# A fifth block product of a first layer computed from sub-blocks, rows fetched whole, and weighting moved from VectorE

## The chip, the cores and the metric

The kernel runs on one core of one Trainium2 chip. The metric is the device time of one execution in microseconds, as the median of several runs. Beside it stands one execution recorded by the hardware profiler, from which all rows here are taken.

## The reference

A batch of 4096 tokens of 512 numbers (`x`) is rotated, routed and sent through a mixture of eight experts, and the result is added back to `x`.

```
x_rotated = hamilton(q_left, hamilton(filter(x), conj(q_right)))   # 4 parts of 128 per token
logits = x_rotated @ gate_w.T ; top 2 of 8 experts, gates from the two scores
disp = each expert's first 1024 tokens, in order (8 x 1024 x 512)
h  = relu(disp @ fc1_w.T + fc1_b)        # 512 -> 2048, per expert
eo = h @ fc2_w + fc2_b                   # 2048 -> 512
out = x + sum over the two choices of gate * eo[expert, place]
```

All of it is float32. Nearly all arithmetic is in the two matrix products of each expert.

## The kernel before, in words

**Blocks.** A prologue on the whole batch finds for every one of the 64 groups of 128 expert slots which token sits in each slot (`slot_tok`), where its result goes (`slot_add`) and where its gates lie (`slot_cho`). After that the work is 32 blocks, k = 0 to 31: expert e = k // 4, and g = k % 4, a quarter of the 2048 hidden units. In a block the first layer makes 512 hidden units for 1024 slots, and the second layer multiplies them by 512 rows of the second weights and adds into the accumulators `acc`.

**Seven products for eight.** Both layers cut each matrix product in 2 by 2 blocks and use a Strassen-like scheme: seven block products, numbered 0 to 6, in place of eight, for which GpSimd and VectorE make sums of blocks ahead (`left1` L132 for weights, `Slots.factors` L772 for tokens, `right2` L177 for second weights, `chain` L810 for hidden units, four VectorE instructions L819, L822, L823, L824). In the first layer (`layer1`, L844) block products 1, 6, 3 and 2 are again made of seven products of their own quarter blocks (`within`, L833, 128x256 each), from sums made by `left_sub` (L146, GpSimd) and `right_sub` (L162, VectorE). They come in pairs (`pair`, L876): PE writes one sub-product of each of two block products into the two halves of a PSUM bank, and VectorE adds both halves to two of the blocks `h11`, `h21`, `r12`, `h22` at once (L890, L903, L909). Block products 0, 5 and 4 are plain there (`half`, L854: four matmuls of 128x512 each, L856). Block 0 (k = 0) is plain in the first layer (`layer1_plain`, L938).

**Order.** The order of instructions is written by hand. `first_layers` (L980) and `second_layers` (L1119) are generators, each of which does one unit of work and yields; a block has 14 units of each. The main loop (L1242) takes one unit of the first layer, calls `turn`, takes one unit of the second layer, calls `turn`. `first_layers` is started ten units earlier, so the second layer of a block runs in the units of the next block. `turn` (L788) pops as many steps from the list `background` as the table `PACE` (L1229) says for that unit, and one step from the list `fetches`. When one generator has ended, `continue` at L1246 skips its `turn`. In the first layer PE's banks come from `ps_1` (four), in the second from `ps_2` (three). Each engine works through its own queue in order.

**Rows in and out.** The tokens of the next expert are fetched by GpSimd as quarters: `gather_quarters` (L706), an indirect DMA of 128 pieces of 512 bytes, 32 of them for an expert, through the table `quarter` (L103, made at L343 to L350, L568 to L576 and L585). They land so that VectorE can turn 32x32 squares of them (`turn_squares`, L725) and rotate them (L768 on ScalarE, L770 on VectorE) as `background`. They begin at (g, i) = (0, 12) and (1, 12), and the rotation at (1, 11) and (2, 9) (L1094, L1096). Results go back per group of 128 slots (`Rows`, L643): `gather_rows` fetches the present rows of `out`, `weigh` (L671, one VectorE instruction L673, 128x512) multiplies `acc` by the gate and adds the row, `scatter` (L675) writes the row by indirect DMA. A gather from `out` that stands behind a scatter into it waits for the scatter. Weights are loaded by SP's queue, `load_w1(k + 1)` and `load_w2(k + 1)` at the start of block k (L1029).

**The end.** After the last block of the first layer only second-layer units are left. There the fetches of `out` rows, the stores of the first four groups and the last matmuls (L1195 to L1206) lie behind one another.

Of the kernel before, what the change touches and what calls it, by code (L numbers as in the profile page):

```python
# [64 lines left out]
def kernel(  # L66
# [36 lines left out]
    quarter = const.tile([P, NS, QT], I32, name="quarter")  # L103
# [96 lines left out]
    with ExitStack() as rctx:  # L200
# [117 lines left out]
        for k in range(K):  # L318
# [24 lines left out]
        spread = rp.tile([P, QT, QT, CW], F32, name="spread")  # L343
        V.tensor_copy(
            spread,
            ident.rearrange("p (q w) -> p q w", w=CW).unsqueeze(2).to_broadcast([P, QT, QT, CW]),
        )
        base = rp.tile([P, 1], F32, name="base")
        for c in range(QT):
            V.memset(base[c * CW : (c + 1) * CW], float(c * N))  # L350

# [216 lines left out]
        quarter_ps = bank(rps, "rank", NT + 1)[:, : QT * NS].rearrange("p (q s) -> p q s", q=QT)  # L568
        for c in range(QT):
            nc.tensor.matmul(  # L570
                quarter_ps[:, c],
                lhsT=spread[:, c].rearrange("p q w -> p (q w)"),
                rhs=tokf,
                start=True,
                stop=True,
            )  # L576

# [6 lines left out]

        V.tensor_scalar(quarter.rearrange("p s q -> p q s"), quarter_ps, base, None, ALU.add)  # L585
# [13 lines left out]
    vp = ctx.enter_context(tc.tile_pool(name="vp", bufs=3))  # L599
# [43 lines left out]
    class Rows:  # L643
# [43 lines left out]
        def store(self, st, acc):  # L687
            self.weigh(st, acc)
            self.scatter(st)

    class Slots:
# [14 lines left out]
        def gather_quarters(self, half, st, q):  # L706

            if q == 0:
                assert self.e == 1 or STORED[half * PER + st] in stored[self.e - 2]
            s = self.e * SLOTS + half * PER + st  # L710
            nc.gpsimd.indirect_dma_start(  # L711
                out=slots_of[half][:, st, q * P : (q + 1) * P],
                out_offset=None,
                in_=xq,
                in_offset=bass.IndirectOffsetOnAxis(ap=quarter[:, s, q : q + 1], axis=0),
            )

        def quarters(self, half):
            return [
                lambda st=st, q=q: self.gather_quarters(half, st, q)  # L720
                for st in range(PER)
                for q in range(QT)
            ]
# [86 lines left out]
    def chain(k, h22):  # L810
# [6 lines left out]
        def last():  # L817
# [6 lines left out]
            lambda: V.scalar_tensor_tensor(r12, r12, 0.0, h11, ALU.max, ALU.subtract),  # L824
            last,
# [18 lines left out]
    def layer1(k, factors, subs):  # L844
# [20 lines left out]
        for m in range(2):  # L865
            half(a[m], m, 0, True)
            nc.scalar.activation(h11[:, m], a[m], AF.Identity, bias=lo[:, m : m + 1])
            yield
        for m in range(2):
            half(a[m], m, 5, False)  # L870
            nc.scalar.activation(r12[:, m], a[m], AF.Identity, bias=lo[:, m : m + 1])
            if m == 1:
                nc.scalar.activation(h21[:, m], a[m], AF.Identity, bias=hi[:, m : m + 1])
            yield

        def pair(n, o, at, base, base_read):  # L876
# [3 lines left out]
            two = h[:, at : at + 2]  # L880
            t, u = bank1(f"t{n}_{k}"), bank1(f"u{n}_{k}")
            halves = t.rearrange("p (n s) -> p n s", n=2)

            def both(bank, i, first=False):
                within(bank[:, A], subs, n, i, first)
                within(bank[:, B], subs, o, i)

            def add(m, half):
                to = two[:, :, m, half]
                V.tensor_tensor(to, halves, to, ALU.add)  # L890

# [344 lines left out]
    with tc.manual_schedule():  # L1236
# [5 lines left out]
        while going:  # L1242
            going = False
            for n, gen in enumerate((first, second)):
                if next(gen, "end") == "end":
                    continue  # L1246
# [51 lines left out]
```

## Time and profile before

| | |
|---|---|
| median of 3 runs | 1574.2 us (1571.47 to 1574.38) |
| the profiled execution's own time | 1572.69 us |
| its span, first to last instruction | 1570.9 us |
| PE (matmuls) busy | 1531.7 us, 98% |
| VectorE (DVE) busy | 1195.8 us, 76% |
| GpSimd (POOL) busy | 1146.5 us, 73% |
| ScalarE (ACT) busy | 280.9 us, 18% |
| mean granted TensorE clock | 0.985 |

The page gives for a group of instructions its line, engine and operation, what is written and read, how many there are, their busy time, the mean duration of one in ns, and after a bar how long the engine stood idle just before them and what ended that. A float32 matmul in the kernel's text appears as two instructions of PE. Matmuls overlap, so a mean duration is longer than the distance between two starts; costs of PE are therefore taken from distances between starts. DMA is the mean busy share of the 16 DMA engines.

### The profile page before, as it was taken

What the parts mean: (1) busy time and instruction counts of PE and PEld (TensorE: products, weight loads), DVE (VectorE), ACT (ScalarE), POOL (GpSimd) and SP (SyncE); (2) the same over time, 40 slices, a digit from 0 to 9 for tenths busy, and PEclk for the clock granted to TensorE, in tenths of its full rate; (3) what the DMA queues carried; (4) which work ended last, traced back from release to release, by engine and by line L of the source; (5) the groups of instructions that cost most, each with busy time, mean ns of one, the idle gap of its engine ahead of it and who ended that gap; (6) DMA issues with size and microseconds to landing.
All of it is one profiled execution on the core that took longest, in us unless ns stands there. A gap on an engine that the chain in (4) does not pass through costs nothing.

```text
span 1570.9 us, 17111 instructions
## 1 busy us (share of the span) xinstructions
PE 1531.7 (98%) x6407; PEld 1191.2 (76%) x6407; DVE 1195.8 (76%) x1667; ACT 280.9 (18%) x390; POOL 1146.5 (73%) x1241
## 2 busy tenths in 40 slices
PE   5899999999999999999999999999999999999995
PEld 3677877877777887777787787787777788778774
DVE  6567887688876788778886888768887688876663
ACT  3222211221112111122111221122111211111100
POOL 1786686876978777887778868687697877764633
PEclk7899999999999999999999999999999999999998
DMA  8452112321321113321043211222132111321002
GB/s 324 158 174 79 55 53 95 104 77 55 110 98 59 63 54 121 113 86 45 20 141 107 81 55 64 85 103 77 54 114 95 64 53 55 121 100 54 28 8 98
DMA packets 48010, 137.46 MB, mean 88 GB/s; under 512 B 9334, under 2 KB 9590, under 8 KB 42808
## 3 DMA queue, kind: packets, MB, share of 16 engines
q1 hardware_dynamic: 22800, 75.54, 13.0%
q0 software_dynamic: 20736, 52.32, 10.5%
q10 hardware_dynamic: 4392, 8.52, 1.4%
q8 instruction: 50, 0.82, 0.2%
q14 instruction: 32, 0.26, 0.1%
HBM read 119.77 MB, written 25.23 MB: 92 GB/s over the span
## 4 chain that ended last, share of the span: by engine, by line
PE 94%; DMA 2%; issue 1%; DVE 1%; POOL 1%; SPq 0%; POOLq 0%; DVEq 0%
PE a L799 27%; PE b L799 20%; PE t L835 14%; PE a L856 14%; PE u L835 7%; PE b L856 7%; PE p L957 2%; PE b L835 2%; PE a L835 2%; DMA xb<-in_xt_dram 1%; DMA rows<-out_dram,slot_tok 1%; POOL rows L622 1%; POOL out_dram L678 0%; DMA rows<-in_x_dram,slot_tok 0%; SPq L216 0%
## 5 line engine op out<-in xcount | busy, mean ns | idle before, releaser
L711 POOL DMA_INDIRECT rows<-in_xq_dram,quarter x224 | 243.4, 1087 | 55.5 <-issue 48.5
L799 PE MATMUL a<-t,hidden 128*128 128x256 f32 x1024 | 243.9, 381 | 9.7 <-DVE v L1185 9.6
L799 PEld LDWEIGHTS a<-t,hidden 128*128 128x128 f32 x1024 | 195.5, 191 | 63.2 <-issue 27.3
L890 DVE TENSOR_TENSOR beside<-t,beside 128x512 f32<-128x512 f32 x248 | 170.2, 686 | 74.7 <-PE t L835 72.5
L831 ACT ACTIVATE beside<-beside 128x1024 f32<-128x1024 f32 x62 | 65.5, 1057 | 583.4 <-DVE beside L890 583.4
L835 PE MATMUL t<-xsub,sub 128*128 128x256 f32 x496 | 127.3, 379 | 0.0
L799 PEld LDWEIGHTS b<-w,hidden 128*128 128x128 f32 x504 | 95.8, 190 | 39.0 <-issue 28.9
L799 PE MATMUL b<-w,beside 128*128 128x256 f32 x512 | 121.0, 379 | 1.5 <-DVE acc L1208 1.5
L799 PE MATMUL a<-w,beside 128*128 128x256 f32 x512 | 121.0, 379 | 0.0
L799 PE MATMUL a<-t,beside 128*128 128x256 f32 x512 | 120.9, 379 | 0.0
L799 PE MATMUL b<-w,hidden 128*128 128x256 f32 x504 | 119.1, 379 | 0.0
L799 PE MATMUL b<-t,hidden 128*128 128x256 f32 x504 | 119.1, 379 | 0.0
L799 PEld LDWEIGHTS b<-w,beside 128*128 128x128 f32 x512 | 97.2, 190 | 28.3 <-issue 16.7
L799 PEld LDWEIGHTS a<-w,beside 128*128 128x128 f32 x512 | 97.3, 190 | 26.5 <-issue 14.8
L856 PE MATMUL a<-x,s 128*128 128x512 f32 x248 | 116.5, 592 | 0.0
L856 PE MATMUL b<-x,s 128*128 128x512 f32 x248 | 116.5, 592 | 0.0
L856 PE MATMUL a<-xa,w 128*128 128x512 f32 x248 | 116.4, 592 | 0.0
L799 PEld LDWEIGHTS a<-t,beside 128*128 128x128 f32 x512 | 97.3, 190 | 13.2
L678 POOL DMA_INDIRECT out_dram<-rows,slot_add x64 | 64.5, 1007 | 57.2 <-DVE rows L673 44.4
L799 PEld LDWEIGHTS b<-t,hidden 128*128 128x128 f32 x504 | 95.8, 190 | 13.0
L835 PEld LDWEIGHTS t<-xsub,sub 128*128 128x128 f32 x496 | 94.2, 190 | 12.8
L137 POOL TENSOR_TENSOR s<-w 128x512 f32<-128x512 f32 x31 | 39.5, 1274 | 79.4 <-PE b L856 79.4
(235 smaller groups left out, 2965.4 us busy)
## 6 DMA issues: line engine op xcount, KB each, us to landing
w<-in_w_dram SPq DMA_DIRECT2D x64, 1024.0 KB, 7.8
xb<-in_xt_dram SPq DMA_DIRECT2D x8, 1024.0 KB, 11.3
out_dram<-in_x_dram ACTq DMA_DIRECT2D x1, 8192.0 KB
rows<-in_xq_dram,quarter POOLq DMA_INDIRECT x224, 2.5
b<-in_b_dram POOLq DMA_DIRECT2D x8, 256.0 KB, 3.9
c<-choice,slot_cho POOLq DMA_INDIRECT x64, 3.4
rows<-out_dram,slot_tok POOLq DMA_INDIRECT x64, 3.7
out_dram<-rows,slot_add POOLq DMA_INDIRECT x64, 2.8
```

Source lines behind the costliest of these rows:

```text
L137: lambda: G.tensor_tensor(s[0], w[:, 1, 0], w[:, 1, 1], ALU.add),
L622: nc.gpsimd.indirect_dma_start(out=t, out_offset=None, in_=src, in_offset=bass.IndirectOffsetOnAxis(ap=slot_tok[:, s : s + 1], axis=0),)
L678: nc.gpsimd.indirect_dma_start(out=out_of[st], out_offset=bass.IndirectOffsetOnAxis(ap=slot_add[:, s : s + 1], axis=0), in_=self.rows[st], ...
L711: nc.gpsimd.indirect_dma_start(out=slots_of[half][:, st, q * P : (q + 1) * P], out_offset=None, in_=xq, in_offset=bass.IndirectOffsetOnAxi ...
L799: nc.tensor.matmul(out[m] if isinstance(out, list) else out[:, m], lhsT=factors[0][n][:, c, (st0 + m) * P : (st0 + m + 1) * P], rhs=factor ...
L831: nc.scalar.activation(h, h, AF.Relu)
L835: nc.tensor.matmul(out, lhsT=subs[0][n][i], rhs=subs[1][n][i], start=first, stop=True, skip_group_check=True,)
L856: nc.tensor.matmul(out, lhsT=factors[0][n][:, c, m * P : (m + 1) * P], rhs=factors[1][n][:, c, :], start=first and c == 0, stop=c == 1, sk ...
L890: V.tensor_tensor(to, halves, to, ALU.add)
L957: nc.tensor.matmul(ps[n][m][:, at], lhsT=w[:, block, i // 2, i % 2, m * P : (m + 1) * P], rhs=x.of(half, i)[:, at], start=i == 0 and at.st ...
```

## The change

1. Block product 5 of the first layer is made of seven products of its quarter blocks, where it was four plain 128x512 matmuls. Its sub-products 1 and 2 (`singles`) go into the bank of product 0, as those of product 6 do; the other five go into a bank of its own, `t5`, and VectorE adds each to `r12` and `h21` at once (`add5`). For this GpSimd makes one more `left_sub` per block and VectorE one more `right_sub` per expert. The first layer's units are cut anew: still 14.
2. Tokens are gathered as whole rows of 2 KB through `slot_tok`, eight indirect DMAs per expert, into the tiles that will hold the rotated tokens (`gather_ahead`); then 48 small DMAs of SP's queue (`exchange`: 16 for the first half, 16 for each two groups of the second) put the pieces in the places that `turn_squares` reads. The table `quarter` and what made it go away. `load_w2(k)` moves from the start of block k - 1 to unit 3 of block k.
3. `store` multiplies by the gate on ScalarE and adds the row on GpSimd.
4. Turns: `PACE` and the starting units are new; the main loop calls `turn` for a generator that has ended too; in the last block two empty steps stand before the fourth step of `chain`. The second layer writes what was in `v2` and `v3` straight into `acc`.

```diff
         def store(self, st, acc):
-            self.weigh(st, acc)
+            nc.scalar.activation(acc, acc, AF.Copy, scale=self.w[:, st : st + 1])
+            r = self.rows[st]
+            nc.gpsimd.tensor_tensor(r, acc, r, ALU.add)
             self.scatter(st)
...
+        def gather_ahead(self, t, half, st):
+            s = self.e * SLOTS + half * PER + st
+            nc.gpsimd.indirect_dma_start(
+                out=t,
+                out_offset=None,
+                in_=xq,
+                in_offset=bass.IndirectOffsetOnAxis(ap=slot_tok[:, s : s + 1], axis=0),
+            )
+        def exchange(self, t, half, at, b):
...
+            for q in range(QT):
+                nc.sync.dma_start(
+                    slots_of[half][
+                        q * CW : (q + 1) * CW, at : at + t.shape[1], b * P : (b + 1) * P
+                    ],
+                    t[b * CW : (b + 1) * CW, :, q * P : (q + 1) * P],
+                )
+        def arrivals(self, half):
+            n = PER if half == 0 else 2
+            t = self.a if half == 0 else self.b
+            for at in range(0, PER, n):
+                for st in range(n):
+                    yield lambda st=st, at=at: self.gather_ahead(t[:, st], half, at + st)
+                yield from [lambda: None] * 2
+                for b in range(QT):
+                    yield lambda b=b, at=at: self.exchange(t, half, at, b)
+                yield from [lambda: None] * 2
...
+            *[lambda: None] * (2 if k == NK - 1 else 0),
             last,
...
+        half(a[0], 0, 0, True)
+        of_bank(h11, 0, lo)
+        yield
+        half(a[1], 1, 0, True)
+        singles(a[0], 5)
+        of_bank(r12, 0, lo)
+        of_bank(h11, 1, lo)
+        of_bank(r12, 1, lo)
+        of_bank(h21, 1, hi)
+        yield
+        t5 = bank1(f"t5_{k}")
+        singles(a[0], 6)
+        of_bank(h21, 0, hi)
+        within(t5[:, A], subs, 5, 0, True)
+        add5(0, A)
+        yield
+        u = bank1(f"u1_{k}")
+        within(t5[:, A], subs, 5, 5)
+        within(t5[:, B], subs, 5, 4)
+        add5(0, B)
+        add5(None, B)
...
+        within(t5[:, A], subs, 5, 6)
+        add5(1, B)
...
+        within(t5[:, A], subs, 5, 3)
+        add5(1, A)
...
-                w1_t, w2_t = load_w1(k + 1), load_w2(k + 1)
+                w1_t = load_w1(k + 1)
+                if k == 0:
+                    loaded[1] = load_w2(1)
...
+                if k > 1 and i == 3:
+                    loaded[k] = load_w2(k)
...
-                    if (g, i) in ((0, 12 if e else 5), (1, 12)):
-                        fetches.extend(nxt.quarters(g))
-                    if (g, i) in ((1, 11), (2, 9)):
+                    if (g, i) in ((0, 12 if e else 5), (1, 8)):
+                        fetches.extend(nxt.arrivals(g))
+                    if (g, i) in ((1, 5), (2, 6)):
                         background.extend(nxt.steps(g - 1))
...
-                if next(gen, "end") == "end":
-                    continue
-                going = True
+                if next(gen, "end") != "end":
+                    going = True
...
-        "xq": x.reshape(N, NJ, 4, 32).transpose(2, 0, 1, 3).reshape(4 * N, P),
+        "xq": x.reshape(N, NJ, 4, 32).transpose(0, 2, 1, 3).reshape(N, D),
```

## The prediction

> **What bounds the kernel now.** First the page: its span, its first part and its chain of work.
>
> ```profile
> span 1570.9 us, 17111 instructions
> ...
> PE 1531.7 (98%) x6407; PEld 1191.2 (76%) x6407; DVE 1195.8 (76%) x1667; ACT 280.9 (18%) x390; POOL 1146.5 (73%) x1241
> ...
> PE 94%; DMA 2%; issue 1%; DVE 1%; POOL 1%; SPq 0%; POOLq 0%; DVEq 0%
> ```
>
> PE is the bound, and all its idle time is 1570.9 - 1531.7 = 39 us. The table of stretches says where that lies.
>
> ```profile
> 0.00:60.00 60.00, 39.15 (x266) 25.72 (x267) 40.98 (x136) 16.72 (x43) 22.76 (x44) 0.74 0.67 253
> 800.00:1000.00 200.00, 200.00 (x826) 156.35 (x825) 157.98 (x212) 35.69 (x46) 153.82 (x165) 1.00 0.24 81
> 1500.00:1571.00 71.00, 52.55 (x222) 43.12 (x220) 37.80 (x58) 3.17 (x3) 22.88 (x20) 0.89 0.18 59
> ```
>
> The numbers are the stretch's length, then busy us of PE, PEld, DVE, ACT and POOL, then PE's clock. In the middle PE never waits, at full clock, and DVE has a fifth of its time free. 21 us of idle time are in the prologue, 18 in the last 71 us. PE's timeline shows block 13 and the end:
>
> ```profile
> 640.55 1.88 PE L856 MATMUL a<-xa,w 128*128 128x512 f32 x4
> 642.27 1.89 PE L799 MATMUL a<-t,hidden 128*128 128x256 f32 x8
> 644.00 1.88 PE L856 MATMUL a<-x,s 128*128 128x512 f32 x4
> ...
> 1546.34 1.89 PE L799 MATMUL a<-t,beside 128*128 128x256 f32 x8
> 1557.79 3.78 PE L799 MATMUL a<-t,hidden 128*128 128x256 f32 x8 [9.56 <-DVE v L1185]
> ```
>
> From start to start, four instructions of 128x512 take 1.72 us (0.43 each) and eight of 128x256 1.73 us (0.216): PE is paid by columns. In the last line PE stands still for 9.6 us. GpSimd's timeline says why:
>
> ```profile
> 1543.12 1.01 POOL L678 DMA_INDIRECT out_dram<-rows,slot_add  x1 [7.33 <-DVE rows L673]
> 1546.13 0.97 POOL L622 DMA_INDIRECT rows<-out_dram,slot_tok  x1 [2.00 <-DMA out_dram<-rows,slot_add]
> 1550.35 1.01 POOL L678 DMA_INDIRECT out_dram<-rows,slot_add  x1 [3.24 <-DMA rows<-out_dram,slot_tok]
> 1553.36 0.97 POOL L622 DMA_INDIRECT rows<-out_dram,slot_tok  x1 [2.01 <-DMA out_dram<-rows,slot_add]
> ```
>
> The last two fetches of rows stand behind stores and wait for those to land; VectorE's weighting waits for the fetches, and the adds that PE needs stand behind it.
>
> **PE's work.** Product 5 of a block goes: 8 instructions of 128x512, 8 x 0.43 = 3.44 us. Seven products of 128x256 come: 14 x 0.216 = 3.02 us. That is 0.43 us (one eighth) for each of 31 blocks: **-13.3 us**, on the path, since PE is full there. The page has as many weight loads as matmuls, of 190 ns each beside 216; 6 more per block stay hidden. The four matmuls for `quarter` end while PE waits for rows in the prologue: nothing.
>
> **VectorE**, whose groups by form are:
>
> ```profile
> L890 DVE TENSOR_TENSOR beside<-t,beside 128x512 f32<-128x512 f32 x248 | 170.2, 686 | 74.7 <-PE t L835 72.5
> L903 DVE TENSOR_TENSOR beside<-u,beside 128x1024 f32<-128x1024 f32 x62 | 75.9, 1225 | 8.8 <-PE u L835 5.8
> L673 DVE SCALAR_TENSOR_TENSOR rows<-acc,w,rows 128x512 f32<-128x512 f32 x60 | 64.9, 1092 | 0.5
> L819 DVE TENSOR_TENSOR hidden<-beside,hidden 128x1024 f32<-128x1024 f32 x32 | 47.6, 1488 | 0.0
> ```
>
> `add5` adds four like L890 and one like L903 per block: 4 x 0.69 + 1.22 = 3.97 us, 123 us in all. `right_sub` adds 32 of about 0.78 (the mean of L170 to L173 on the same kind of tile): 25 us. The 60 weightings that leave take 65 away. In sum +83 us, 1279 of some 1555 us: 82%, not the bound on the whole. Unit by unit (a unit of both layers is 3.4 us of PE), the demand overruns only in units 3 and 5, by 1 us at most, and is worked off in the next.
>
> What matters is one place. Before, units 0 to 3 had no VectorE work of the first layer, so the four instructions of `chain` lay free there. Now PE's second write into `t5` (unit 3) needs `add5(0, A)` (unit 2), which stands behind the last of the chain. Counting from the end of PE's last matmul of the block before: PE reaches that write after 1.72 + 1.72 + 1.72 + 2.59 + 1.72 + 1.29 + 1.72 = 12.5 us. VectorE, in order, with the mean durations (L822 1.73, L823 1.28, L824 1.59, L819 1.49, second-layer adds when PE gives them), starts L819 at 10.3, ends at 11.8, ends `add5` at 12.45. With L819 at its shortest, 1.21, there are 0.3 us to spare; at its longest, 1.98, 0.5 us are missing.
>
> Here a rule of the Trainium skill speaks against the change: "SBUF — State Buffer", section "Who interferes with whom", says that a VectorE instruction with two SBUF inputs and a GpSimd instruction that reads SBUF take the shared port by exclusive lock, the loser blocking for the other's whole length. The chain's instructions are such; GpSimd gets more such work (below). The spread of L819, 1.21 to 1.98, fits. By the rule, with each of the four meeting one GpSimd add of 1.27 us, the chain would be 4.9 + 5.1 = 10 us and the write about 2 us late in every block; by the rows the four sum to 6.1 us, 1.2 above their shortest. I follow the rows, with some more meetings: 0.1 us per block, **+3 us**; ends 0 and 22 (all four at or near their longest: 0.7 us x 31). A gain is excluded, since PE waited for nothing there.
>
> **GpSimd.** Leaving: 224 quarter fetches, 243 us. Coming: 56 row fetches at 1.02 (as L622), 57 us; 124 small adds (as L155 to L158 on `s`, 2.46 per four), 76 us; 60 row adds of 128x512 at about 1.27, 76 us. In sum -34 us. But they bunch: in block g = 0 of an expert, stores, fetches and `left_sub` come together from unit 9 on. Working that queue through from unit 9 (1.3 us per DMA with its gap, 1.27 per add, two waits for ScalarE), the last of the four row fetches is issued 24.5 us later, some 10 us after the block's end. Three things stand behind it. `left_sub` of product 5 is in front of most, done 4 us before its use. `right2` of the next second layer is done with 2.7 us to spare. The third is the exchange: fetch landed 3.5 us after issue (median of L622's transfers 3.7), then 16 DMAs by SP at 0.38 us each (the smallest load, of 32 KB, took SP 0.38) = 6 us, then about 2 us to land (that load: 1.7). In all 36 us from unit 9, where VectorE comes to `turn_squares` at about 35; behind that no add is needed by PE for another 3 us or so. So it is hidden, barely: 0, ends 0 and 21 (3 us x 7). SP's weight loads queued behind the exchange are needed a block later. If that cover were gone, each us would cost 7.
>
> **ScalarE** gets 60 x 0.69 = 41 us, at 18% busy. The new reads between `singles` 5 and 6 have a second-layer unit of 1.72 us before them against 0.9 needed: 0.
>
> **Start.** Block 1 runs its units 0 and 1 without second-layer units. Between `singles` 5 and 6 PE then waits some 0.9 us for ScalarE; VectorE has the chain and eight `right_sub` instructions there, about 3 us behind in units 3 to 5, which gives PE about 1 us more. **+2 us**; ends 0 and 5 (the exchange runs while DMA is 0.6 busy).
>
> **End.** Since `turn` now goes on for the ended generator, all eight row fetches come twice as fast and before the first store. They start where they do now (1527.3) and are issued by 1538, landed by 1542 (in the old times). The 9.6 us wait of PE goes. Next late is GpSimd: from 1543.1 four row adds and four stores, 4 x (1.3 + 1.3) = 10.4, to 1553.5, plus 1 for the lock; then four stores 1.27 apart, the last starting at 1558.3 where it is 1566.8: **-8.5 us**; ends -10 and -6. The two empty steps keep the chain's order; L824 now stands before the add L1131, which shifts a stall of 1.5 us that is there already.
>
> **Sum:** -13.3 - 8.5 + 2 + 3 = -16.8 us; the profiled execution's 1572.69 gives 1555.9. That run lay 1.5 below the median of 1574.2, from which the sum gives 1557.4. I say 1557.
>
> **Rivals.** (a) Nothing stalls: PE's 13.3 and the full 10 at the end, 1 lost at the start: 1574 - 22 = 1551. For it: the overruns by unit are small. 20%. (b) The exchange comes late by some us beyond its cover in each expert, since row adds meet the lock: 7 x 1.3 = 9 us more, 1566. For it: the count of 36 against 35. 14%. (c) The end doesn't shorten, because GpSimd's four row adds take the place of the waits: 1574.2 - 13.3 + 5 = 1566. Against it: the fetches are clearly in front now. 8%. (d) Slower: the first add of `t5`, behind L819 in every block. Price: each us by which the chain is longer. It decides from 20 / 31 = 0.65 us per block; at the four maxima of the rows it is 0.7: -13.3 - 8.5 + 2 + 22 = +2, and with the exchange late as well by a few us, 1579. 8%. The forecast, 50%.
>
> Faster by over 0.2% (about 3 us, what a measurement can tell from none): 0.88, that is all but (d) and a little of (b) and (c); within 0.2%: 0.05; slower 0.07. The range reaches to (a) and into (b): 1549 to 1567.
>
> **What would show it.** Per block, 16 matmul instructions of 128x512 in the first layer instead of 24, and a period of 46.1 us instead of 46.56 (the chain of work lists the same product at 126.83 and 173.39). PE idle before L856 or the `t5` matmuls with VectorE's `add5` as releaser would show (d); VectorE idle before the transpose, released by a DMA of `xa`, shows (b). At the end, no row fetch behind a store, and the last store bound by GpSimd. The forecast is wrong if PE is not full between 130 and 1500, or if the end keeps a wait for rows.

## The result, and the profile after

| | before | after |
|---|---|---|
| median | 1574.25 us (4 runs) | 1660.12 us (4 runs, 1659.41 to 1661.06) |
| ratio, 95% interval | | 1.055 [1.0537, 1.0563] |
| span of the profiled execution | 1570.9 us | 1658.7 us |
| mean granted clock | 0.985 | 0.971 |

The kernel became slower by 86 us, where the forecast was 17 us faster. The page of the changed kernel, its span, its busy times and the first line of its chain of work:

```profile
span 1658.7 us, 18203 instructions
...
PE 1553.5 (94%) x6585; PEld 1234.7 (74%) x6585; DVE 1297.1 (78%) x1788; ACT 312.6 (19%) x450; POOL 1113.9 (67%) x1257
...
PE 58%; DVE 15%; POOL 12%; issue 6%; SPq 4%; DMA 4%; another core or an unknown queue 1%; POOLq 0%; DVEq 0%
```

The busy times of VectorE (1297) and GpSimd (1114) are near the forecast's 1279 and 1112. But the chain that ended last was 94% PE and is now 58%, with VectorE, GpSimd and SP's queue in it: work that used to lie beside PE now stands in front of it.

Where that happens is seen when the starts of each block are read off PE's timeline (the first matmul `a<-xa,w` of a block) and their distances are compared with those of before, which were 46.56 us for every block but the first two. Block k is quarter g = k % 4 of its expert; the last column runs from block 31's start to the end of the span.

| us beyond the kernel before | block 1 | g = 0 (7 blocks) | g = 1 (7) | g = 2 (8) | g = 3 (7) | from block 31 on |
|---|---|---|---|---|---|---|
| changed kernel | +18.9 | +21.8 | +42.1 | +7.2 | +2.5 | -4.2 |

With -0.5 ahead of block 1 these make the 87.8 us between the two spans. Four places matter.

**g = 1: the rotation waits for the exchange.** VectorE, SP and PE in block 13, one timeline each:

```profile
703.57 1.22 DVE L881 TENSOR_TENSOR beside<-u,beside 128x1024 f32<-128x1024 f32 x1 [0.17 <-PE u L833]
711.74 0.73 DVE L723 STREAM_TRANSPOSE xps<-rows 128x512 f32<-128x512 f32 x1 [6.95 <-DMA rows<-xa]
```
```profile
699.69 10.38 SPq L703 DMA_DIRECT2D rows<-xa  x16
```
```profile
705.96 1.89 PE L796 MATMUL a<-t,beside 128*128 128x256 f32 x8
713.10 1.22 PE L833 MATMUL t<-xsub,w 128*128 128x256 f32 x2 [5.25 <-DVE beside L876]
714.97 3.62 PE L796 MATMUL a<-w,beside 128*128 128x256 f32 x8
```

VectorE comes to the transpose at 704.8 and stands there for 6.95 us, since SP took 10.38 us to issue the 16 DMAs of the exchange, 0.65 us each; the last landed 1.7 us later. Behind the transpose in VectorE's queue is the add that empties the bank for PE (L876), so PE waits 5.25 us. And after such a wait PE is slow: eight matmuls take 3.62 us instead of 1.89. The table of stretches over the same time (columns as in the forecast; the share behind the clock is DMA's):

```profile
700.00:708.00 8.00, 7.85 (x37) 6.57 (x35) 3.58 (x5) 0.00 (x0) 7.35 (x9) 1.00 0.55 123
708.00:713.00 5.00, 0.00 (x0) 0.00 (x0) 1.26 (x3) 0.50 (x1) 4.52 (x6) 0.95 0.82 219
713.00:719.00 6.00, 5.90 (x13) 4.54 (x14) 2.40 (x5) 2.98 (x5) 5.29 (x8) 0.50 0.47 178
719.00:723.00 4.00, 4.00 (x14) 2.50 (x13) 2.16 (x4) 0.00 (x0) 1.92 (x4) 0.96 0.46 131
```

The granted clock is 0.50 for about 6 us after the wait, which costs another 3 us. Block 13 lasts 54.7 us: 8.1 more than before, of which 5.25 are the wait and about 3 the clock. The Trainium skill ("TensorE: Matmul & The Clock Gate", Part 1) says that the clock falls to half after an idle window of some 3.4 us. The waits alone, 42.0 us in the table of waits for seven of them, block 1's among them, don't make the 61 us that these blocks lost. The clock in the 7 us behind each wait makes most of the rest; here for blocks 5 and 9:

```profile
316.60:323.60 7.00, 7.00 (x21) 5.19 (x22) 3.36 (x6) 2.90 (x5) 6.17 (x9) 0.76 0.53 182
515.20:522.20 7.00, 7.00 (x16) 4.93 (x17) 2.59 (x4) 2.86 (x5) 6.42 (x11) 0.56 0.52 178
```

It is 0.56 behind the waits of blocks 9 and 13 (5.66 and 5.25 us), 0.76 to 0.80 behind those of the other four (4.26 to 4.62), and 0.73 in block 1. Seven us times what is missing to 1 gives 3.1 us, 1.4 to 1.7, and 1.9: 14.5 in all. What is left are smaller waits, 3.3 us of them in block 1 and 1.95 (for an L890) in block 29, the seventh block of g = 1, behind which no expert comes and which has no exchange. In all six exchange blocks, with waits of over 3.4 us, the clock fell as the skill says. The rows go further than the rule, though. In g = 0 PE waits only 2.3 us; the stretch after that wait, in blocks 8 and 12:

```profile
450.00:455.00 5.00, 5.00 (x18) 4.04 (x17) 3.53 (x8) 0.00 (x0) 4.30 (x7) 0.70 0.63 201
650.00:655.00 5.00, 5.00 (x25) 4.40 (x24) 4.90 (x10) 0.00 (x0) 4.29 (x7) 1.00 0.67 205
```

The clock falls in the first and not in the second. That is why the blocks of g = 0 last either 48.7 or 50.4 us.

**Block 1: the exchange waits for a copy.** SP's timeline shows the 16 DMAs of block 1 as one row of 22 us. The table of waits of SP's queue shows what is in it:

```profile
93.11 21.99 SPq L703 DMA_DIRECT2D rows<-xa  x16
```
```profile
SPq L703 <- DMA out_dram<-in_x_dram: 11.6, 1, 11.6
```

Seen in shorter windows, SP issues six DMAs in 3.96 us from 93.11 on and ten in 6.38 us from 108.72 on, 0.65 us each as in the other blocks. Between them it stands for 11.6 us until the copy of `x` into `out` has landed, 8 MB that ScalarE's queue issued at 57.68 (the kernel before has that copy too). The exchange reads nothing of it. In the packed trace the copy and the seventh DMA of the exchange have the same semaphore number, which may be the tie; no run tested it. VectorE's first transpose waited 14.2 us in this block and PE 13.2.

**g = 0: the first add of `t5` behind the chain.** VectorE's and PE's timelines at the start of block 12 (it starts at 635.25):

```profile
636.78 1.16 DVE L172 TENSOR_TENSOR xsub<-x 128x256 f32<-128x256 f32 x1
637.86 2.28 DVE L819 SCALAR_TENSOR_TENSOR hidden<-beside,hidden 128x1024 f32<-128x1024 f32 x1
640.07 0.68 DVE L1187 TENSOR_TENSOR v<-a,acc 128x512 f32<-128x512 f32 x1
640.67 1.69 DVE L820 TENSOR_TENSOR hidden<-hidden,beside 128x1024 f32<-128x1024 f32 x1
642.28 1.49 DVE L173 TENSOR_TENSOR xsub<-x,xsub 128x256 f32<-128x256 f32 x1
643.69 1.47 DVE L821 SCALAR_TENSOR_TENSOR beside<-beside 128x1024 f32<-128x1024 f32 x1
645.09 0.68 DVE L1262 TENSOR_TENSOR acc<-a,acc 128x512 f32<-128x512 f32 x1
645.69 2.10 DVE L816 TENSOR_TENSOR hidden<-beside,hidden 128x1024 f32<-128x1024 f32 x1
647.71 0.68 DVE L890 TENSOR_TENSOR beside<-t,beside 128x512 f32<-128x512 f32 x1
```
```profile
648.44 1.13 PE L833 MATMUL t<-xsub,sub 128*128 128x256 f32 x4 [2.26 <-DVE beside L890]
```

VectorE never rests here. L819, L820, L821 and L816 are the chain (L822, L823, L824 and L819 of before), L890 is `add5(0, A)`, and PE's second write into `t5` waits for it. In every g = 0 block this wait is 2.26 to 2.28 us; in seven of the eight g = 2 blocks the same wait is 0.6. L172 and L173 between the chain's instructions are the last two `right_sub` instructions of product 5.

**The end** gives 4.2 us instead of the 8.5 foreseen. VectorE's and PE's timelines there:

```profile
1636.40 7.31 DVE L652 SCALAR_TENSOR_TENSOR rows<-acc,w,rows 128x256 f32<-128x256 f32 x6
```
```profile
1644.36 3.63 PE L796 MATMUL a<-t,hidden 128*128 128x256 f32 x8 [5.15 <-DVE acc L1239]
```

The fetches are ahead of all stores, as foreseen. But six weightings that stand in front of the add which PE needs take 7.31 us, 1.22 each, where they took 0.48 before. GpSimd's row adds run at the same time; "5 plain, mended" below shows that they are the cause.

### The profile page after: what moved, and what is told of

It reads as the page before. It is cut to its first block, busy times and chain, and to the rows that moved or that the text cites. A ratio compares the mean times of both kernels' runs of the same rounds, so it can differ in the third digit from the quotient of the medians.

```text
span 1658.7 us, 18203 instructions
## 1 busy us (share of the span) xinstructions
PE 1553.5 (94%) x6585; PEld 1234.7 (74%) x6585; DVE 1297.1 (78%) x1788; ACT 312.6 (19%) x450; POOL 1113.9 (67%) x1257
## 4 chain that ended last, share of the span: by engine, by line
PE 58%; DVE 15%; POOL 12%; issue 6%; SPq 4%; DMA 4%; another core or an unknown queue 1%; POOLq 0%; DVEq 0%
PE a L796 18%; PE t L833 13%; PE b L796 10%; PE b L854 6%; PE u L833 5%; SPq L703 4%; DVE hidden L819 2%; POOL out_dram L657 2%; PE a L854 2%; POOL xa L690 2%; DVE hidden L816 2%; DVE beside L890 2%; POOL rows L669 2%; DVE hidden L820 1%; DMA xa<-in_xq_dram,slot_tok 1%
## 5 line engine op out<-in xcount | busy, mean ns | idle before, releaser
L833 PE MATMUL t<-xsub,sub 128*128 128x256 f32 x682 | 183.4, 388 | 26.0 <-DVE beside L890 24.0
L876 DVE TENSOR_TENSOR beside<-t,beside 128x512 f32<-128x512 f32 x248 | 169.6, 684 | 42.2 <-PE t L833 39.0
L833 PEld LDWEIGHTS t<-xsub,sub 128*128 128x128 f32 x682 | 124.5, 190 | 62.0 <-DVE beside L890 40.6
L864 ACT ACTIVATE beside<-a,b_sb 128x512 f32<-128x512 f32 x186 | 117.6, 688 | 163.0 <-PE a L833 115.5
L796 PE MATMUL a<-w,beside 128*128 128x256 f32 x512 | 128.8, 397 | 0.0
L890 DVE TENSOR_TENSOR beside<-t,beside 128x512 f32<-128x512 f32 (+1 forms) x155 | 122.2, 788 | 7.4 <-PE t L833 4.7
L796 PEld LDWEIGHTS a<-w,beside 128*128 128x128 f32 x512 | 103.6, 202 | 28.8 <-issue 14.3
L796 PE MATMUL b<-w,beside 128*128 128x256 f32 x512 | 124.4, 387 | 0.6 <-DVE acc L1262 0.6
L140 POOL TENSOR_TENSOR s<-w,s 128x512 f32<-128x512 f32 x31 | 40.4, 1302 | 121.5 <-PE t L833 121.2
L796 PEld LDWEIGHTS a<-t,beside 128*128 128x128 f32 x512 | 97.3, 190 | 13.2
## 6 DMA issues: line engine op xcount, KB each, us to landing
xb<-in_xt_dram SPq DMA_DIRECT2D x8, 1024.0 KB, 10.2
```

The source lines that it names most:

```text
L140: lambda: G.tensor_tensor(s[3], w[:, 0, 1], s[1], ALU.subtract),
L796: nc.tensor.matmul(out[m] if isinstance(out, list) else out[:, m], lhsT=factors[0][n][:, c, (st0 + m) * P : (st0 + m + 1) * P], rhs=factor ...
L833: nc.tensor.matmul(out, lhsT=subs[0][n][i], rhs=subs[1][n][i], start=first, stop=True, skip_group_check=True,)
L864: nc.scalar.activation(to[:, m], a[m], AF.Identity, bias=bias[:, m : m + 1])
L876: V.tensor_tensor(to, bank.rearrange("p (n s) -> p n s", n=2), to, ALU.add)
L890: V.tensor_tensor(to, term.to_broadcast(shape), to, ALU.add)
```

## Experiments

Times are medians; each ratio is to the kernel before on the same chip (1573.0 to 1574.7 us). The columns are as above, in us beyond the kernel before.

| kernel | median | ratio [95%] | block 1 | g = 0 | g = 1 | g = 2 | g = 3 | from block 31 |
|---|---|---|---|---|---|---|---|---|
| changed | 1660.1 | 1.0550 | 18.9 | 21.8 | 42.1 | 7.2 | 2.5 | -4.2 |
| rotation later | 1602.7 | 1.0185 [1.0168, 1.0202] | 10.4 | 20.8 | 1.2 | -0.3 | 1.3 | -4.1 |
| store by VectorE | 1632.0 | 1.0362 [1.0344, 1.0379] | 20.6 | 31.1 | 9.2 | 7.3 | 2.5 | -10.2 |
| product 5 plain | 1608.9 | 1.0228 [1.0211, 1.0245] | 21.1 | 0.0 | 16.0 | 2.1 | 0.8 | -4.1 |
| `t5` later | 1651.3 | 1.0490 [1.0473, 1.0508] | 18.8 | 13.3 | 45.5 | 3.9 | 2.0 | -3.8 |
| before, with the new end | 1561.8 | 0.9923 [0.9909, 0.9936] | 0 | 0 | 0 | 0 | 0 | -11.7 |
| rotation later, 5 plain | 1579.5 | 1.0039 [1.0027, 1.0051] | 8.6 | 0.0 | 1.9 | 0.0 | 0.0 | -4.3 |
| rotation and `t5` later | 1594.6 | 1.0128 [1.0112, 1.0143] | 11.0 | 4.9 | 3.1 | 4.4 | 3.9 | -3.9 |
| all that, store by VectorE | 1606.9 | 1.0210 [1.0196, 1.0224] | 2.8 | 12.6 | 20.4 | 5.8 | 4.0 | -10.0 |
| two queues | 1693.5 | 1.0757 [1.0739, 1.0775] | 17.8 | 21.7 | 76.9 | 9.6 | 2.5 | -4.0 |
| rotation and `right_sub` later | 1588.2 | 1.0086 [1.0069, 1.0103] | 10.3 | 6.1 | 2.9 | 1.4 | 1.3 | -4.0 |
| rotation and `last` later | 1597.4 | 1.0148 [1.0131, 1.0165] | 11.2 | 8.7 | -0.4 | 6.6 | 4.6 | -4.4 |
| mended | 1591.2 | 1.0113 [1.0096, 1.0130] | 2.5 | 16.0 | -0.4 | 7.2 | 4.7 | -10.4 |
| half the exchange | 1618.6 | 1.0288 [1.0272, 1.0304] | 12.8 | 24.9 | 3.7 | 7.4 | 2.5 | -4.0 |
| 5 plain, mended | 1565.8 | 0.9961 [0.9948, 0.9975] | 1.0 | 0.0 | 1.9 | 0.0 | 0.0 | -10.0 |

In the expectations, "theory X" is that the exchange comes late, "theory Y" that the chain (and the port that VectorE and GpSimd share) delays the adds of `t5`.

**Rotation later.** The rotation of the first half starts at unit 8 of g = 1 instead of unit 5; two empty turns of g = 2 are used so that it ends in time.

```diff
-                    if (g, i) in ((1, 5), (2, 6)):
+                    if (g, i) in ((1, 8), (2, 6)):
...
-        [(1, 1)] * 3 + [(0, 0), (0, 1), (1, 1), (0, 0), (0, 1)] + [(1, 1)] * 3 + [(0, 1), (1, 1), (0, 0)],
+        [(1, 1)] * 3 + [(0, 1), (0, 1), (1, 1), (0, 1), (0, 1)] + [(1, 1)] * 3 + [(0, 1), (1, 1), (0, 0)],
```

> The changed kernel, but the rotation of the next expert's first half starts three units later, at unit 8 of block g = 1 (two more background steps in blocks g = 2 and 3 keep it in time). Nothing else moves: exchange and fetches are issued where they were. Theory X (the exchange lands late, VectorE stands at its first transpose of exchanged rows, and PE's adds stand behind it): the blocks g = 1 fall from 52.3 to 55.1 us to about 47.6, the first block from 62 to about 50, in all about -50: 1610 us. Theory Y (the loss is the port lock: the four chain instructions on VectorE run longer beside GpSimd, and the adds of t5 behind them come late in every block): no change, 1655 to 1662.

Measured: 1602.7, 57 us less; g = 1 from +42.1 to +1.2. The table of waits of VectorE has one line for the transposes; first the changed kernel, then this one (total, number, longest):

```profile
DVE xps L723 <- DMA rows<-xa: 53.1, 7, 14.2
```
```profile
DVE xps L723 <- DMA rows<-xa: 5.8, 1, 5.8
```

Only block 1's is left. Six of the seven g = 1 blocks last 46.5 us; the rest of the +1.2 is block 29. That is the largest cause, and g = 0 with its 2.36 us waits hasn't moved: two causes, in different places.

**Store by VectorE.** `store` weights and adds the row on VectorE again.

```diff
         def store(self, st, acc):
-            nc.scalar.activation(acc, acc, AF.Copy, scale=self.w[:, st : st + 1])
-            r = self.rows[st]
-            nc.gpsimd.tensor_tensor(r, acc, r, ALU.add)
+            self.weigh(st, acc)
             self.scatter(st)
```

> The changed kernel with the weighting and adding of stored rows back on VectorE; fetch, exchange and the fifth product stay. Theory X: the four row adds no longer stand before the four row fetches on GpSimd, so fetches and exchange come about 6 us earlier and VectorE's wait of 7 us nearly goes in the six experts that have stores before them, but not in the first block: about -40, 1620 us. Theory Y: the lock is lighter only in blocks g = 0 and at the end: -5 to -10, about 1652.

Measured: 1632.0. GpSimd's queue is shorter by the row adds (the last row fetch of an exchange is issued 8.1 us after the start of the g = 1 block instead of 12.1), and the transposes wait 19.8 us in all, 15.2 of them in block 1, instead of 53.1; g = 1 loses 9 us instead of 42; the end falls to -10.2, as PE's wait there shrinks to 0.82 us. But g = 0 gets worse by 9 us: VectorE has the weightings as well, PE waits another 0.47 us in each of these blocks for an add of VectorE, and the clock falls in one block more.

**Product 5 plain.** The first layer is the one of before; rows, exchange and stores as changed.

> The changed kernel with block product 5 plain again (four matmuls of 128x512, no t5, no left_sub and right_sub for it); fetch, exchange, stores and turns stay as changed. Theory Y: blocks g = 0, 2 and 3 go back to 46.56 us each, which gives back about 40 us of waits and costs 13 of matmuls: about 1632; blocks g = 1 keep their wait for the exchange. Theory X alone (no loss at t5): 13 us more than the changed kernel, 1673.

Measured: 1608.9. g = 0 is at 46.6 us, so its loss is product 5's alone. The expectation for Y was missed by 23 us in its favour, but for another reason: g = 1 fell from +42.1 to +16.0. Without product 5 the six transposes of g = 1 still wait 26.7 us in all (38.9 in the changed kernel), but of each wait of some 4.5 us only 1.6 to 2.6 reach PE, and the clock falls in two of the six blocks only. The two causes are tied together: without product 5 GpSimd has fewer `left_sub` adds in front of the fetches, and the last of them is issued 9.4 us after the start of the block instead of 12.1.

**`t5` later.** `t5` is first written in unit 3 instead of 2, behind the single writes into `u`.

> The changed kernel with the first writes of t5 one unit later (unit 3 in place of 2; the sub-products 1 and 2 of block product 1 take its place; the same instructions, still 14 units). Theory Y: the chain has 3 us more before an add that PE needs, so the waits at t5 of 0.6 to 2.3 us go: blocks g = 0, 2, 3 fall to about 46.3, -30 us, about 1630. Theory X alone: 1655 to 1662.

Measured: 1651.3, 9 us less. g = 0 gains 8.5 and keeps a wait of 1.4 us; the delay was put off more than taken away.

**Before, with the new end.** The kernel before with two edits of the change:

```diff
-                if next(gen, "end") == "end":
-                    continue
-                going = True
+                if next(gen, "end") != "end":
+                    going = True
...
+            *[lambda: None] * (2 if k == NK - 1 else 0),
             last,
```

> The kernel before, with only the change at the end: turn goes on for the generator that has ended, and two empty steps stand ahead of the last instruction of the last chain. In the changed kernel the last 45 us became 39 us, and its weightings there were slow beside GpSimd's row adds. Here VectorE weights the rows and GpSimd has no row adds. Theory that the adds cost the rest of the forecast gain: the end shortens by the full 8 us or more, 1566. Theory that the end is bound by the row of fetches and stores in any case: 6 us or less, 1568 to 1570.

Measured: 1561.8, 11.3 us faster, and the fastest kernel of all here: 0.9923 of before. GpSimd's waits for the DMAs of rows are gone; PE's wait in front of the last matmuls is

```profile
1549.47 1.99 PE L799 MATMUL a<-t,hidden 128*128 128x256 f32 x8 [0.85 <-DVE v L1186]
```

where it was 9.56. So the new end is worth 11. GpSimd's row adds beside the weightings take 6 of them back in the changed kernel, as the runs show in which VectorE adds the rows at the end (-10.0 to -10.4 against -3.8 to -4.4 in the last column).

**Rotation later, 5 plain.**

> Rotation three units later and product 5 plain, everything else as changed: row fetches, exchange, ScalarE and GpSimd stores, the end. If the two causes (the late exchange; the adds of t5 behind the chain) are all of the loss, the blocks go back to 46.6 us as before, block 1 keeps some 10 us of loss, and the end brings 6: 1574.6 + 10 - 6 = 1579. If GpSimd's row adds cost more by the port lock than these two waits show, blocks of g = 0 stay at 47 us or more: 1585 to 1595.

Measured: 1579.5, as the first theory said, but with some luck: block 1 lost 8.6 instead of 10, the end brought 4.3 instead of 6, and g = 1 lost 1.9 that the theory hadn't. Blocks of g = 0, 2 and 3 last 46.6 us: gathering whole rows, SP's 48 DMAs per expert and the stores of ScalarE and GpSimd cost a block nothing once the rotation waits for nothing, and give it nothing either. Against "rotation later" this is product 5 alone: 1602.7 - 1579.5 = 23 us that the seven products cost, where 13 were to be gained.

**Rotation and `t5` later**, with the two `right_sub` instructions moved as well.

```diff
-                later(right_rest, (0, 1))
+                later(right_rest, (3, 4))
```

> Rotation three units later; t5 written one unit later; and the last two right_sub instructions of product 5, which stand among the chain in units 0 and 1 of g = 0, in units 3 and 4. Theory that the loss of g = 0 (48.8 to 50.5 us, a PE wait of 2.36 us) is the chain's place ahead of the first add of t5: the wait goes, g = 0 falls to 46.5 us, 7 x 3 = 21 us less than with the later rotation alone: 1582. Theory that GpSimd's adds lock VectorE out for so long that the delay only moves to the next write: g = 0 stays at 48 us or more, 1595 to 1602.

Measured: 1594.6. g = 0 comes from +20.8 to +4.9, as expected; but PE now waits 0.7 to 0.85 us for an L890 in the blocks of g = 0, 2 and 3 and 0.3 in g = 1, and g = 1 to 3 lose 11 us together. The first theory's 1582 was missed by 13; the time is beside the second's 1595 to 1602, but with g = 0 at 47.3 and not at 48 or more. The place of the two instructions was a cause, as a later run with that edit alone confirms. `t5` in a later unit makes a new wait; that its adds there meet those of `t1` is the likely reason, not a tested one.

**All that, store by VectorE**, and the first expert's rotation five units later.

> As the last kernel, and the weighting and adding of rows at a store is VectorE's again (as before the change), and the first expert's rotation starts five units later than in the changed kernel. Theory of two waits and a lock: no wait of over 1 us is left, blocks near 46.3 us, the end 8 us shorter than before, block 1 a few us longer than before: 1560 to 1566, faster than both kernels. Theory that VectorE, at over 80%, becomes the next bound: blocks of g = 0 at 47.5 us or more, 1575 or more.

Measured: 1606.9, a clear miss of the theory of waits alone. The second theory, VectorE as the bound, is the nearer one (48.4 us in g = 0). The largest loss is in g = 1, though, where PE waits 2.2 us at a write into `t5` in six blocks and the clock falls behind three of these waits. Block 1 comes down to +2.8 and the end to -10.0.

**Two queues.** Half of the exchange's DMAs are issued by ScalarE's queue.

```diff
-                nc.sync.dma_start(
+                (nc.sync if q % 2 else nc.scalar).dma_start(
```

> The changed kernel with half of the exchange's DMAs issued by ScalarE's queue instead of SP's. SP took 10.4 us for 16 of them, 0.65 each, and VectorE's transpose waited up to 7 us for the last. Theory that the issue time of one queue makes the exchange late: two queues take 5.2 us, the waits in g = 1 go, with the fall of the clock behind each: g = 1 near 47 to 48 us, block 1 some 8 us shorter, 1610 to 1620. Theory that the transfers themselves are late (fetch, landing): no change, 1655. A third way: ScalarE's queue stands at its first exchange DMA until the rows have landed, and PE waits for its activations: any time above 1620, with PE released by ScalarE.

Measured: 1693.5, the third way. ScalarE's timeline in block 13:

```profile
711.74 2.67 ACTq L703 DMA_DIRECT2D rows<-xa  x4
714.45 0.69 ACT L864 ACTIVATE beside<-a,b_sb 128x512 f32<-128x512 f32 x1 [11.08 <-DMA rows<-xa]
```

ScalarE's first DMA stands until the rows have landed and 2 us more (SP's first went out at 709.61), and the read of PE's bank (L864) behind it is 11 us late; PE then waits 10.2 to 10.7 us in each g = 1 block that has an exchange. SP's eight took 5.12 us, again 0.64 each.

**Rotation and `right_sub` later.** Against "rotation later" only this:

```diff
-                later(right_rest, (0, 1))
+                later(right_rest, (2, 3))
```

> Rotation three units later, and of the rest of the change only the last two right_sub instructions of product 5 moved from units 0 and 1 (among the chain) to 2 and 3, in g = 0; t5 where the change has it. With the later rotation alone: 1603, g = 0 at 48.8 to 50.5, PE wait 2.36 us. Theory that these two instructions, 1.5 us each beside GpSimd's adds, are what makes the chain late in g = 0 alone: g = 0 falls to 46.5 to 46.8, 1603 - 7 x 3 = 1582 to 1585. Theory that the chain is late by itself there: the wait stays above 1 us, 1592 or more.

Measured: 1588.2. Two instructions per expert, moved by two units, are worth 14.5 us: g = 0 from +20.8 to +6.1, PE's wait from 2.36 to 0.68, and the clock, which fell in three of these blocks, stays up. A rest of the wait stays, so 3 us more than the first theory said.

**Rotation and `last` later.** The last instruction of the chain stands behind the adds of `t5` in unit 3.

> Rotation three units later, and the last instruction of each chain (2.1 us beside GpSimd's adds) placed behind the three adds of t5 in unit 3, instead of ahead of the first. Everything else as changed. Theory that the first add of t5 waits only for the chain: 2.1 us of the 2.36 go in g = 0, and the 0.2 to 0.6 us that are left over 46.17 in the other blocks too: g = 0 at 46.5, others 46.2 to 46.4, 1603 - 7 x 3.2 - 23 x 0.25 = 1575. Theory that PE's instructions as such take the time that is left in g = 1 to 3 (46.4 to 46.8): those stay, 1580.

Measured: 1597.4, another miss. g = 1 stays at 46.5, but in the others PE's writes into `t5` wait 0.3 to 0.8 us for one add or the next. The table of stretches shows how full VectorE is there: 20 us from the start of a g = 0 block of the kernel before, of a g = 3 block of the same kernel, and of a g = 0 block of "rotation later" (from 1.7 us behind its start):

```profile
590.56:610.56 20.00, 20.00 (x78) 14.62 (x77) 18.27 (x23) 4.32 (x7) 18.96 (x17) 1.00 0.39 145
730.23:750.23 20.00, 20.00 (x78) 14.62 (x77) 18.44 (x22) 4.33 (x7) 18.05 (x19) 1.00 0.32 105
```
```profile
609.20:629.20 20.00, 17.64 (x78) 14.31 (x77) 19.68 (x25) 3.80 (x6) 18.37 (x19) 1.00 0.36 115
```

VectorE (third busy time) was already at 18.3 of 20 us before, with GpSimd at 19 beside it, and is now at 19.7. That leaves little room for the 4 us of `add5`, and moving one instruction moves the wait. But fullness isn't all: g = 3 was as full before and lost only 0.4 us per block by the change, and moving the two `right_sub` instructions helped g = 0 more than this edit. What stands in front of the first add counts as well.

**Mended**: all of these together, and VectorE weighting the rows in the last block alone.

> All of it together: the chain's last instruction behind the adds of t5, right_sub later, rotation three units later (five in the first expert), and VectorE weighting the rows in the last block. Theory of the waits: blocks of 46.2 to 46.4 us, block 1 at 46, the end 11 us shorter than before as in the run of the tail alone: 1573 - 11 - 29 x 0.25 + 3 = 1558, faster than the kernel before and than the tail alone. Theory that something not seen yet holds the blocks at 46.5 or more: 1562 to 1570, no better than the tail alone.

Measured: 1591.2. The end is at -10.4 and block 1 at +2.5 as expected; g = 0 is at 48.9 us with a wait of 1.67. The theory of waits was wrong for product 5: with `last` moved as well, g = 0, 2 and 3 lose 28 us, where "rotation and `right_sub` later" lost 9. That kernel with this run's block 1 and end was not run; by the table it would be near 1588 - 8 - 6 = 1574, an estimate, and so no faster than the kernel before.

**Half the exchange.** Only 8 of each 16 DMAs are made, so half of the pieces aren't brought to their places.

```diff
-            for q in range(QT):
+            for q in range(2):
```

> The changed kernel with only 8 of each 16 DMAs of the exchange; half of the pieces of the gathered rows aren't brought to their places, so the numbers that follow are others, and the work of the engines is the same. Theory that SP's time per DMA (0.65 us, not the 0.38 of the sum) is what makes the exchange late: 5.2 us less before the transposes, the 5.3 us waits in g = 1 go, with the fall of the clock behind each; block 1 loses 8 to 12 us less. Near the run with the later rotation: 1605 to 1615. Theory that the fetch of the rows is late by itself, and the issue of 16 DMAs has little part in it: 1640 or more.

Measured: 1618.6. SP's timeline and VectorE's waits:

```profile
679.02 5.10 SPq L703 DMA_DIRECT2D rows<-xa  x8
```
```profile
DVE xps L723 <- DMA rows<-xa: 17.6, 7, 8.3
```

The issue takes half as long, the waits fall from 53.1 to 17.6 us, and g = 1 from +42.1 to +3.7. In g = 1 it is SP's time per DMA that makes most of the lateness, not the fetch; in block 1 the wait for the copy stays, as the seventh DMA is still among the eight. (The time is a little above what was expected, as g = 0 stays at 50.) Three of the seven g = 1 blocks now last 46.1 us. Half the DMAs are half the transfers too, but in the changed kernel VectorE's transpose starts 1.6 to 1.8 us behind SP's last DMA in every exchange, so the transfers keep up with SP.

**5 plain, mended.**

> Product 5 plain, rotation three units later (five in the first expert), VectorE weighting the rows in the last block, the rest as changed. The run with the plain product and the later rotation gave 1579.5, with 51.7 us in block 1 and a PE wait of 5.2 us at the end. Theory that these two are all that is left: block 1 at 45 us (-7), the end 5 us shorter, 1567 to 1569, between the tail alone (1561.8) and the kernel before. If gathering whole rows were of use by itself, it would be at or below the tail alone, 1562 or less.

Measured: 1565.8, 1 us below the expected 1567 to 1569. The weightings of 128x256 at the end, first in "rotation later, 5 plain", where GpSimd adds rows beside them, then here, where it doesn't:

```profile
L652 DVE SCALAR_TENSOR_TENSOR rows<-acc,w,rows 128x256 f32<-128x256 f32 x8 | 8.2, 1082 | 0.0
```
```profile
L652 DVE SCALAR_TENSOR_TENSOR rows<-acc,w,rows 128x256 f32<-128x256 f32 x8 | 3.4, 479 | 0.0
```

The end goes from -4.3 to -10.0 with it. All parts of the change but product 5, put where they don't wait, are faster than before by the new end alone, and slower than that end by itself.

## Why the prediction was wrong

**PE's work, -13.3 us: right in size, but not reached.** Where nothing waits a block lasts 46.1 us (half the exchange, g = 1), which is the forecast's 46.13. In the changed kernel no group of blocks comes to that.

**The exchange, hidden: the step that failed first.** The forecast said "16 DMAs by SP at 0.38 us each (the smallest load, of 32 KB, took SP 0.38) = 6 us". In g = 1 they took 10.4: all rows at hand were loads from DRAM, and these DMAs go from one place of SBUF to another over 32 partitions. The other terms can be laid beside block 13, counted from the end of block 12 (683.97). The forecast's last fetch, 24.5 us from unit 9, was "some 10 us after the block's end", so its 36 us for the last piece are 21.5 here and its 35 for VectorE 20.5. VectorE came to the transpose at 20.8, as foreseen. The last row fetch was issued by 12.1 instead of 10, and the last piece had landed at 27.8. Of these 6.3 us, 4.4 are SP's time and some 2 are GpSimd's queue. The cover, "no add is needed by PE for another 3 us or so", was 1.7. The forecast had seen the mechanism and how thin the cover was, gave its end as 21 us and the rival (b) 9; the early rotation cost 57. What the sum lacked besides was the clock: the waits of 4.3 to 5.7 us brought 1.4 to 3.1 more, a term that stood nowhere; in g = 0, too, waits of 2.3 us brought 1.7 more in four of seven blocks.

**The chain and `t5`: "starts L819 at 10.3, ends at 11.8, ends `add5` at 12.45", the second failed step.** PE's side of it was exact: in block 12 PE came to the write at 646.02 (644.29, where the unit before it starts, and its 1.73), 12.5 us after the first layer's last matmul of the block before, which ended at 633.53. VectorE's `add5` ended at 648.39, after 14.9, so 2.4 us late. Two things were missing. The list of what lies among the chain left out the two `right_sub` instructions which the change itself puts into units 0 and 1 of g = 0, 1.16 and 1.49 us in block 12; moving them gave back 14.5 us. And the chain was taken at its mean over all blocks, 6.1 us, though each g has its own: 2.28 + 1.69 + 1.47 + 2.10 = 7.5 in g = 0. Together these are 4.1 us, more than the 2.4, presumably since VectorE no longer waits for PE in between. The trace of before already spoke against the 11.8; in its block 12, which starts at 590.55, VectorE has:

```profile
595.93 1.49 DVE L170 TENSOR_TENSOR xsub<-x 128x256 f32<-128x256 f32 x1
597.35 2.29 DVE L824 SCALAR_TENSOR_TENSOR beside<-beside 128x1024 f32<-128x1024 f32 x1
...
600.16 1.41 DVE L819 TENSOR_TENSOR hidden<-beside,hidden 128x1024 f32<-128x1024 f32 x1
```

The same count begins there at 588.83, a unit of 1.72 ahead of the block. A `right_sub` (L170) lies among the chain, L819 ends at 601.57, after 12.7 us, and by the same count an add behind it would have been 0.9 us late with nothing else added.

The chain's instructions read two operands in SBUF and lie beside GpSimd's adds for the next second layer. That the rule of the shared port, which the forecast cited, lengthened them is the likely reading: in the changed kernel the adds with one operand in PSUM (L876) all lie between 0.67 and 0.69 us, the chain's instructions of 128x1024 between 1.21 and 3.55. A run without GpSimd's adds beside the chain wasn't made; for the weightings at the end there is one (1.08 to 0.48 us). The 2 us per block that the forecast put down to the rule and set aside would have been nearer than its 0.1 for g = 0, though not for g = 2 (0.6); its own figures, a chain of 10 us instead of 6.1, would rather make 3.9. Rival (d), "the first add of `t5`, behind L819 in every block", was the right mechanism for g = 0; it got 8% and a price of 0.7 us per block, where the seven blocks of g = 0 paid 2.3 and more.

**VectorE, "82%, not the bound on the whole".** True, and no help. That "the demand overruns only in units 3 and 5, by 1 us at most" doesn't fit the measured stretch: VectorE had 1.7 us free in the first 20 us of a g = 0 block before the change, and `add5` and the two `right_sub` instructions bring 4.0 and 2.7 us.

**The end, -8.5: the order was right, a size was not.** The fetches moved ahead and alone they are worth 11.3. The term "plus 1 for the lock" should have been some 6: the forecast counted GpSimd's row adds as longer, and not VectorE's weightings beside them, which went from 0.48 to 1.22 us.

**Start, +2:** it was 18.9, of which 15 are the exchange in block 1: 13.2 us of PE's wait and 1.9 of slow clock. (PE's wait for ScalarE was 0.9 us as foreseen, that for VectorE 1.9 instead of 1.) The sum had the exchange there at nothing, with "the exchange runs while DMA is 0.6 busy" for its end of 5; what it met was SP's wait of 11.6 us for the copy of `x`.

**ScalarE, GpSimd's sum, the row gathers:** 0 each, and right where the rotation has time, as "rotation later, 5 plain" shows with blocks of 46.6 (46.9 in g = 1). Where it has none, the row adds in front of the fetches count, as "store by VectorE" shows.

In sum, going from before: +6 for rows, exchange and stores with a later rotation (block 1 +8.6, end -4.3, g = 1 +1.9), +23 for product 5 in that kernel, +57 for the early rotation. Open are what ties the exchange of block 1 to the copy of `x`, and how much of the chain's length is the port.

## What to carry to other kernels

Ask of each engine how full it is in the stretch where the new work goes, not on the whole, and list in its order every instruction that lies there, those of the change itself too. When a wait can reach a few microseconds, price the slow clock behind it (here 1.4 to 3.1 us behind waits of 4.3 to 5.7). A transfer with a cover of 3 us is not hidden when its duration is borrowed from another kind of DMA, and a row that merges many DMAs can hide a wait: ask what the queue waited for. Before a change of many parts is built, try the small one by itself: here the end alone was worth 11.3 us, more than the 8.5 that the forecast gave it.

## What was not expected of the hardware

- SP took 0.65 us to issue each 64 KB DMA from SBUF to SBUF over 32 partitions, 0.64 with eight instead of 16 in a row, and 0.63 for one of 32 KB (six in 3.78 us); weight loads of 1 MB took it 0.33 to 0.54 in the blocks.
- A queue that issues DMAs stood for 11.6 us in front of one of them until an 8 MB copy of another queue, of whose data it used nothing, had landed.
- After a wait of 5.25 us TensorE ran at a clock of 0.50 for 6 us; after a wait of 2.27 us it was 0.70 for the next stretch in one block, after one of 2.26 it stayed at 1.00 in another.
- A VectorE instruction of two SBUF operands of 128x256 took 0.48 us without GpSimd's 128x512 adds and 1.22 beside them; one of 128x1024 took 1.21 at the least and, in the chain of block 12, 2.28.
